# A hybrid block on one core: residual additions moved to TensorE and ScalarE, and other costs in the kernel's planner

## Chip, core and metric

The kernel runs on one core of one Trainium2 chip. The metric is the device time of one execution in microseconds (us), as the median of several runs. TensorE is called PE below, VectorE DVE, ScalarE ACT, GpSimd POOL, and SP is the engine that only issues transfers.

## What is computed

The input x is 8 sequences of 512 tokens of 128 features, float32. The reference, cut to its frame:

```python
def reference(x, ...):
    x = x + delta_rule_attention(layernorm(x))   # "a": 16 heads of 8, short convolution, recurrence over time
    x = x + experts(layernorm(x))                # "f": top 2 of 8 experts, 128 -> 256 -> 128, relu
    x = x + linear_attention(layernorm(x))       # "b": elu+1 features, causal, chunked
    x = x + experts(layernorm(x))                # "g": the same weights as f
    return x
# experts:
#   topw, topi = top_k(softmax(x @ Wg), 2); topw = topw / sum(topw)
#   out = sum over the two chosen e of topw[e] * (relu(x @ W1[e]) @ W2[e])
```

All of it is in float32 except where only signs or counts matter.

## The kernel before

Time is cut into eight chunks of 64 steps; a chunk holds 512 tokens (8 sequences by 64 steps) and lives in SBUF as a tile `x_a` of 128x4x128 values, the residual stream of that chunk. Every chunk passes through four parts: `prepare` and the recurrence (names ending in `_a`, `st`, `pj`, `terms`, `po`), then the experts f, the linear attention b and the experts g. Four lanes work on different chunks at once. Chunk 7 is cut in two halves of 256 tokens.

The experts (`moe`) sort rows: each row is scaled for its two experts (`m_xw`) and sent by indirect transfers from POOL to the table `there` in HBM, ordered by expert. Blocks of 128 rows come back (`m_xs`), are turned by PE (`s_pt`), multiplied with the weights of their expert (`s_ph`, ACT's relu into `hT`, `y_py`) and stored to the table `back`. Then two sets of four indirect gathers bring the two results of every row into two tiles `m_g` (128x512 each), and DVE adds each to `x_a`. The two halves of chunk 7 and one part, g of chunk 6, use all experts for all rows instead (`all_experts`) and gather nothing. So there are 13 parts that gather: 7 of f and 6 of g.

The projections of both attentions end in `add_projected`: PE multiplies with Wo into a PSUM bank `s_po`, with a product of a row of ones for the bias in b, and DVE adds the bank to `x_a`.

The program is one straight stream per engine. Its order is not written by hand: `Weaver` is a planner that runs while the program is built. Each part is a generator, a stream, that says before each step which engine it wants next; the planner keeps a clock for every engine, adds the time that `duration` gives for each instruction, and picks, among the steps that could start soonest, the one with the largest value of `chains` (how long before the end the step must start) plus `FAVOURED` (a hand-set bonus by part and chunk). `AHEAD_OF` says how much later than the earliest a step may start and still be picked. `PLANS` and `PASSES` run the planner several times without issuing anything, to make `chains`. What the planner believes is thus never a wait in the program; it decides the order on each engine.

There is one thing more that the planner writes into the program. Where it believes that PE is going to be idle, `keep_busy` fills most of the gap with products of ones that nobody reads (`busy`, 128x512, bf16):

```python
if gap < 0.6 or not banks.free:
    return
...
n = int(BUSY * gap / 0.22)        # BUSY = 0.7
```

Each engine executes its stream in order, so such a product stands in front of whatever comes next on PE. What `duration` says of PE (`took(engine, us, lag)` takes the time on the engine and the lag until another engine sees the result) is therefore also what decides how many of them there are.

Of the kernel before, what the change touches and what calls it, by code (L numbers as in the profile page):

```python
# [14 lines left out]
ALU = mybir.AluOpType  # L15
# [4 lines left out]
P = 128  # L20
# [19 lines left out]
PREPARED_ON_POOL = ()  # L40
VALUES_ON_POOL = ()
ADDED_ON_PE = ()
AHEAD_OF = 0
PLANS = 4

LANDS = 3.4
ROWS_LAND = 3.8

PASSES = (
    (1, 0.0, {}),  # L50
    (35, 0.1, {}),
)

FAVOURED = {
    ("b", 0): 365, ("b", 3): 20, ("b", 4): 25, ("b", 5): -8, ("b", 6): -10, ("b", 7): -22, ("b", 7.5): 10,
    ("beside",): -5,
    ("ending",): 4,
    ("f", 0): -43, ("f", 1): 17, ("f", 2): -3, ("f", 3): -3, ("f", 4): -3, ("f", 5): 15, ("f", 6): 309, ("f",
    7): -32, ("f", 7.5): 29,
    ("g", 0): -5, ("g", 3): -13, ("g", 4): -37, ("g", 5): -2, ("g", 6): -15, ("g", 7): 321, ("g", 7.5): 170,  # L60
    ("prepare", 0): -5, ("prepare", 1): -2, ("prepare", 2): -22, ("prepare", 3): 10, ("prepare", 5): -6,
    ("prepare", 7): -10,
    ("recur", 0): 105, ("recur", 1): 98, ("recur", 2): -19, ("recur", 3): -7, ("recur", 4): 10, ("recur", 5):
    -47, ("recur", 6): 15, ("recur", 7): -28,
    ("values",): 14,
}

HALVED = (7,)
# [28 lines left out]
class Weaver:  # L97
# [69 lines left out]
    def spawn(self, steps, part=None):  # L167

        ended = Event()

        def run():
            yield from steps
            ended.at, ended.causes = self.seen(), self.waited()

        of = self.stream
        self.live.append(Stream(self.state(), (of.key, of.spawned), part or of.part, run()))
        of.spawned += 1
        return ended
# [154 lines left out]
class Timed:  # L333
# [5 lines left out]
    def __getattr__(self, op):  # L339
        call = getattr(self.engine, op)  # L340

        def issue(*args, **kw):
            r = call(*args, **kw)  # L343
            self.weaver.took(*duration(self.key, op, args, kw))
            return r

        return issue


def free_size(ap):  # L350
    n = 1
    for d in ap.shape[1:]:
        n *= d
    return n


def duration(key, op, args, kw):
    if op == "dma_start":
        return key, 0.4, 0.0, None, LANDS
    if op == "value_load":  # L360
        return key, 0.75, 0.0
    if op == "indirect_dma_start":
        return key, 1.3, 0.0, None, ROWS_LAND
    if key == "PE":
        if op == "transpose":
            return key, 0.2, 0.15
        return key, max(free_size(args[2]) * 1.75e-3, 0.27), 0.15
    out = args[0] if args else kw["out"]
    n = free_size(out)
    if op == "tensor_reduce":  # L370
        n = free_size(args[1])
    if key == "ACT":
        table = TABLE_OF.get(args[2]) if op == "activation" else None
        return key, (0.39 if "bias" in kw else 0.2) + n * 0.76e-3, 0.1, table
    if key == "POOL" and ALU.pow in args:
        return key, 1.05, 0.1
    if key == "POOL":
        return key, 0.15 + n * (1.8e-3 if n > 512 else 2.2e-3), 0.1
    if op == "reciprocal":
        return key, 0.15 + n * 6.5e-3, 0.0  # L380
    if op == "bn_stats":
        return key, 0.28, 0.0
    return key, 0.16 + n * 1.04e-3, 0.0
# [3 lines left out]
def kernel(ctx: ExitStack, tc: tile.TileContext, *tensors: bass.AP):  # L387
# [9 lines left out]
    for n, ahead, favoured in PASSES:  # L397
        for _ in range(n):
# [3 lines left out]
            chains.update(weaver.before_end())  # L402
    merged(ctx, tc, Weaver(chains, FAVOURED, AHEAD_OF), *tensors)


def merged(
# [40 lines left out]
    spawn = weaver.spawn  # L447
    pe = Timed(weaver, nc.tensor, "PE")
    dve = Timed(weaver, nc.vector, "DVE")
    act = Timed(weaver, nc.scalar, "ACT")  # L450
# [25 lines left out]
    ident = const.tile([P, P], F32, name="ident")  # L476
# [38 lines left out]
    def by_row(at):  # L515
        return None if isinstance(at, Shape) else bass.IndirectOffsetOnAxis(ap=at, axis=0)
# [16 lines left out]
    def held_in(n, shape, key, pool_=slots):  # L533
        return Slots(weaver, pool_, shape, key, n)

    banks = held_in(GENERAL, [P, 512], "s", ps)
# [101 lines left out]
    def all_of(events):  # L638
        for e in events:
            yield e  # L640
# [587 lines left out]
    def moe(xt, name, tag):  # L1228
# [7 lines left out]
        held, m_ = helds[own], ms[own]  # L1236
        pl = yield from long_banks.take(f"pl_{name}")
        yield "PE"
        for j in range(nb):
            pe.matmul(  # L1240
                pl[:, j * (NE + 1) : (j + 1) * (NE + 1)], xnT[:, j * P : (j + 1) * P], wg,
                start=True, stop=True,
# [191 lines left out]
        for g in range(0, NBK, 4):  # L1434
            n = min(4, NBK - g)
# [48 lines left out]

            stored.append(spawn(put()))
        yield from all_of(stored)
        added = []
        for k in range(2):
            g = yield from m_.take(f"g_{name}_{k}")
            for at in range(HB):  # L1490
                yield "POOL"
                pool.indirect_dma_start(
                    out=g[:, at, :], out_offset=None, in_=yd,
                    in_offset=by_row(rows[:, k * HB + at : k * HB + at + 1]),
                )
                back = weaver.now
                weaver.now -= ROWS_LAND

            def add(g=g, back=back):
                weaver.goes_on(back)  # L1500
                yield "DVE"
                dve.tensor_tensor(xt, xt, g, ALU.add)
                m_.give(g)

            added.append(spawn(add()))
        yield from all_of(added)
        sets.give(own)

    def add_projected(xt, lhsT, w, name, bias=None):
        nb = xt.shape[1]  # L1510
        po = yield from banks.take(f"po_{name}")
        yield "PE"
        whole = name in ADDED_ON_PE
        rows = xt.rearrange("p b d -> p (b d)")
        if whole:
            pe.matmul(po[:, 0 : nb * D], ident, rows, start=True, stop=False)
        if bias is not None:
            pe.matmul(
                po[:, 0 : nb * D].rearrange("p (b d) -> p b d", b=nb), ones1,
                bias.unsqueeze(1).to_broadcast([1, nb, D]), start=not whole, stop=False,  # L1520
            )
        start = not whole and bias is None
        for j in range(nb):
            pe.matmul(
                po[:, j * D : (j + 1) * D], lhsT[:, j], w, start=start, stop=start or j + 1 == nb
            )
        if whole:
            yield "ACT"
            act.copy(rows, po[:, 0 : nb * D])
        else:  # L1530
            yield "DVE"
            dve.tensor_tensor(rows, rows, po[:, 0 : nb * D], ALU.add)
        banks.give(po)
# [127 lines left out]
    def linear_attention(c, lo, xt, tag):  # L1661
        nb = xt.shape[1]
        n = f"b{c}_{lo}"
        if c > 0:
            yield from all_of([fired("att", c - 1, i) for i in rows_of(c - 1)])
        xnT_ = yield from xns.take(f"xnT_{n}")
        xnT = xnT_.rearrange("p b d -> p (b d)")
        yield from transposed(xt, xnT, n)
        pm = yield from banks.take(f"pm_{n}")
        yield "PE"  # L1670
        for j in range(nb):
            pe.matmul(
                pm[:, j : j + 1], xnT[:, j * P : (j + 1) * P], wg[:, NE:], start=True, stop=True
            )
        mean = small.tile([P, HB], F32, tag="mean" + tag, name=f"mean_{n}")[:, 0:nb]
        yield "ACT"
        act.copy(mean, pm[:, 0:nb])
        banks.give(pm)
        rs = yield from inverse_deviation(xt, mean, n, tag)
        nrs = small.tile([P, HB], F32, tag="nrs" + tag, name=f"nrs_{n}")[:, 0:nb]  # L1680
        yield "POOL"
        pool.tensor_scalar(nrs, rs, -1.0, None, ALU.mult)

        att = yield from xns.take(f"att_{n}")
        fire("att", c, lo)
        yield from all_of([spawn(attend(c, lo, j, xnT, rs, nrs, att)) for j in range(nb)])
        yield from transposed(att[:, 0:nb], xnT, f"t_{n}")
        xns.give(att)
        yield from add_projected(xt, xnT_, wob, f"b{c}" if nb == HB else n, bob)
        xns.give(xnT_)  # L1690
# [16 lines left out]
    def of_rows(c, lo, nb, tag):  # L1707

        n = f"{c}" if nb == HB else f"{c}_{lo}"
        part = c + lo / HB  # L1710
        xt = xts[c][:, lo : lo + nb]
        yield ("f", part)
        yield from add_projected(xt, oTs[c][:, lo : lo + nb], woa, f"a{n}")
        fire("added", c, *([] if nb == HB else [lo]))
        yield from moe(xt, f"f{n}", tag)
        yield ("b", part)
        yield from linear_attention(c, lo, xt, tag)
        yield ("g", part)
        yield from moe(xt, f"g{n}", tag)
        yield "SP"  # L1720
        for i in range(2):
            sp.dma_start(in_units(out, c, i)[:, lo : lo + nb], xt[i * CH : (i + 1) * CH])
# [71 lines left out]
```

## Time and profile before

| | |
|---|---|
| median of 3 runs | 951.38 us (951.37 to 951.84) |
| the profiled execution | 1007.78 us, its span 1006.1 us |
| mean granted PE clock in the profile | 0.919 |
| busy: PE, PE weight loads, DVE, ACT, POOL | 83%, 54%, 65%, 52%, 47% of the span |
| instructions | 14877, of them 4144 products on PE, each with its weight load |
| `busy` products | 514 |

The profiled execution is longer than the median run: 1007.78 against 951.38. Durations below are of the profiled execution, from its first to its last instruction. A float32 product is two instructions on PE, a transpose or a bf16 product is one. The busy time of PE counts each product from its start to its modelled end, so a product that is followed closely by another is counted in part while the next already runs: what a product takes away from others is seen better in the distance between starts. The instructions of the program nearly all carry the line of one helper (L343), so groups are told apart by the names of their tiles; the `busy` products have a line of their own, L1735.

### The profile page before, as it was taken

The page shows a single profiled execution, that of the slowest core. Times are in us where ns is not written, and L with a number is a line of the kernel's source. Part 1 is how long each engine was busy: PE and PEld are TensorE (multiplying, and loading weights), DVE is VectorE, ACT ScalarE, POOL GpSimd, SP SyncE. Part 2 cuts the span into 40 slices and gives each one's busy share as a digit, 9 for nine tenths or more (in the row PEclk, how much of TensorE's full clock was granted, in tenths as well). Part 3 has the DMA queues.
Part 4 walks back from the last instruction along what each step waited for, and adds up shares of the span by engine and source line. Part 5 has one row for each costly group of instructions (what it writes and reads, how often), then busy time and mean ns, then how long its engine had stood idle before and what let it go on. Part 6 is the DMA issues. An engine that isn't in the chain of part 4 may idle for free.

```text
span 1006.1 us, 14877 instructions
## 1 busy us (share of the span) xinstructions
PE 834.4 (83%) x4144; PEld 540.9 (54%) x4144; DVE 655.4 (65%) x1625; ACT 523.7 (52%) x1464; POOL 476.3 (47%) x615
## 2 busy tenths in 40 slices
PE   8978697688898887888787788779876848999998
PEld 3332242537453676447643575547745737776566
DVE  1377878648898487788788796688774812264520
ACT  4343255665656456765385475753752526435343
POOL 1133136254646434774367635774366442554530
PEclk9989799799899789899988898989998969999999
DMA  1404504586206464367615574763635636611111
GB/s 27 101 21 116 159 6 127 159 228 189 57 4 178 126 204 129 96 174 222 164 53 161 161 223 126 197 190 102 202 113 155 201 107 169 170 54 48 37 48 38
DMA packets 157989, 126.83 MB, mean 126 GB/s; under 512 B 53105, under 2 KB 123730, under 8 KB 157906
## 3 DMA queue, kind: packets, MB, share of 16 engines
q1 hardware_dynamic: 150674, 112.16, 39.6%
q0 software_dynamic: 6656, 13.64, 4.7%
q8 instruction: 33, 0.54, 0.2%
q14 instruction: 50, 0.41, 0.1%
q10 hardware_dynamic: 576, 0.08, 0.0%
HBM read 91.70 MB, written 36.23 MB: 127 GB/s over the span
## 4 chain that ended last, share of the span: by engine, by line
PE 37%; DVE 28%; ACT 11%; issue 7%; DMA 5%; POOL 5%; another core or an unknown queue 4%; SPq 2%; ACTq 0%; DVEq 0%; POOLq 0%
PE s_ph_g L343 5%; PE y_py_g L343 5%; PE y_py_f L343 4%; PE s_pc_b L343 4%; PE s_pu_b L343 3%; PE s_ph_f L343 3%; DVE st L343 3%; ACT squares L343 3%; DVE factors L343 3%; PE s_pp_a L343 2%; POOL po L343 2%; DVE terms L343 2%; SPq L343 2%; DVE pj L343 2%
## 5 line engine op out<-in xcount | busy, mean ns | idle before, releaser
L1735 PE MATMUL busy<-ones 128*128 128x512 bf16 x514 | 131.5, 403 | 5.3 <-DVE sbd L343 2.4
L343 POOL TENSOR_TENSOR po<-st,kq 128x256 f32<-128x256 f32 x128 | 94.8, 768 | 5.7 <-DVE o L343 5.5
L343 PE MATMUL s_pp_a<-xnT_a,wc 128*128 128x512 f32 x192 | 92.6, 621 | 0.6 <-ACT xnT_a L343 0.6
L343 POOL COPY st<-st 128x64 f32<-128x64 f32 x31 | 8.0, 257 | 175.9 <-DVE st L343 165.5
L1735 PEld LDWEIGHTS <-ones 128*128 128x128 bf16 x514 | 52.1, 104 | 71.3 <-issue 27.2
L343 POOL TENSOR_TENSOR kv_b<-ph_b,v 128x1024 f32<-128x1024 f32 x32 | 63.1, 1974 | 56.8 <-DVE ph_b L343 31.7
L343 PE MATMUL y_py_f<-wt_f,hT_f 128*128 128x128 f32 x420 | 64.7, 308 | 21.5 <-ACT hT_f L343 19.7
L343 ACT ACTIVATE hT_g<-s_ph_g 128x512 f32<-128x512 f32 (+1 forms) x96 | 48.5, 511 | 62.8 <-PE s_ph_g L343 38.2
L343 DVE TENSOR_REDUCE st<-terms 128x64 f32<-128x320 f32 x128 | 62.1, 485 | 24.8 <-ACT terms L343 7.9
L343 ACT COPY terms<-st 128x64 f32<-128x64 f32 x128 | 39.5, 309 | 74.5 <-DVE st L343 64.8
L343 PE MATMUL s_pc_b<-kv_b,tri 128*128 128x512 f32 x128 | 69.7, 648 | 10.3 <-POOL kv_b L343 6.7
L343 PEld LDWEIGHTS y_py_f<-wt_f,hT_f 128*128 128x128 f32 x420 | 58.6, 218 | 28.0 <-ACT hT_f L343 23.6
L343 POOL DMA_INDIRECT there<-m_xw_f,rows_f x56 | 55.9, 999 | 34.2 <-ACT m_xw_f L343 17.6
L343 ACT ACTIVATE hT_f<-s_ph_f 128x512 f32<-128x512 f32 (+1 forms) x88 | 43.7, 501 | 52.8 <-PE s_ph_f L343 38.7
L343 POOL DMA_INDIRECT m_g_f<-back,rows_f x56 | 56.1, 1002 | 31.3 <-issue 15.1
L343 PE MATMUL y_py_g<-wt_g,hT_g 128*128 128x128 f32 x360 | 50.3, 288 | 20.9 <-issue 11.1
L343 DVE TENSOR_REDUCE o<-po 128x64 f32<-128x512 f32 x64 | 42.9, 679 | 34.5 <-POOL po L343 34.5
L343 PE MATMUL s_ph_f<-xsT_f,wt_f 128*128 128x128 f32 x420 | 60.7, 298 | 5.5 <-ACT xsT_f L343 4.5
L343 DVE TENSOR_REDUCE factors<-pj 128x32 f32<-128x288 f32 x128 | 58.8, 460 | 7.4 <-ACT factors L343 3.8
L343 PEld LDWEIGHTS s_ph_f<-xsT_f,wt_f 128*128 128x128 f32 x420 | 56.5, 211 | 10.5 <-ACT xsT_f L343 6.3
L343 PEld LDWEIGHTS s_pp_a<-xnT_a,wc 128*128 128x128 f32 x192 | 36.2, 198 | 43.8 <-issue 37.7
L343 PE MATMUL s_ph_g<-xsT_g,wt_g 128*128 128x128 f32 x360 | 52.2, 296 | 9.0 <-ACT xsT_g L343 3.4
(312 smaller groups left out, 1989.3 us busy)
## 6 DMA issues: line engine op xcount, KB each, us to landing
wt_f<-w SPq DMA_DIRECT2D x105, 256.0 KB
wt_g<-w SPq DMA_DIRECT2D x90, 256.0 KB
scr<-y_a SPq DMA_DIRECT2D x24, 256.0 KB
m_xs_f<-there SPq DMA_DIRECT2D x21, 256.0 KB
back<-yb_f SPq DMA_DIRECT2D x21, 256.0 KB
m_xs_g<-there SPq DMA_DIRECT2D x18, 256.0 KB
back<-yb_g SPq DMA_DIRECT2D x18, 256.0 KB
qk<-scr SPq DMA_DIRECT2D x16, 256.0 KB
```

What stands on the lines that cost most here:

```text
L343: r = call(*args, **kw)
L1735: nc.tensor.matmul(pt, ones, ones.unsqueeze(1).to_broadcast([P, 4, P]), start=True, stop=True)
```

## The change

`add_projected` always adds the residual rows by a product with the identity into the same bank, ahead of the others, and ACT copies the bank back to `x_a`. In `moe` both gathers are awaited together; then PE adds `x_a` and both gathered tiles by three products with the identity into a bank `s_pg`, and ACT copies it to `x_a`. The planner gets other costs for PE: 0.9 ns for a column instead of 1.75, a least time of 0.05 us instead of 0.27, a transpose like a product of 128 columns (0.115 us instead of 0.2), widths between 128 and 256 taken as 256, and a lag of 0.3 us instead of 0.15. `AHEAD_OF`, `PASSES` and `FAVOURED` have other values.

```diff
-AHEAD_OF = 0
+AHEAD_OF = 0.15
@@
 PASSES = (
     (1, 0.0, {}),
-    (35, 0.1, {}),
+    (17, 0.0, {}),
 )
 
 FAVOURED = {
-    ("b", 0): 365, ("b", 3): 20, ("b", 4): 25, ("b", 5): -8, ("b", 6): -10, ("b", 7): -22, ("b", 7.5): 10,
...
-    ("values",): 14,
+    ("b", 5): 159, ("b", 6): -3, ("b", 7): 28, ("b", 7.5): 27,
...
+    ("recur", 0): 74, ("recur", 1): 36, ("recur", 4): 2, ("recur", 7): 1,
+    ("values",): -5,
 }
@@ def duration(key, op, args, kw):
     if key == "PE":
-        if op == "transpose":
-            return key, 0.2, 0.15
-        return key, max(free_size(args[2]) * 1.75e-3, 0.27), 0.15
+
+        n = P if op == "transpose" else free_size(args[2])
+        n = 2 * P if P < n < 2 * P else n
+        return key, max(n * 0.9e-3, 0.05), 0.3
@@ def moe(xt, name, tag):
-        added = []
+        both = []
         for k in range(2):
             g = yield from m_.take(f"g_{name}_{k}")
             for at in range(HB):
...
-                back = weaver.now
                 weaver.now -= ROWS_LAND
-
-            def add(g=g, back=back):
-                weaver.goes_on(back)
-                yield "DVE"
-                dve.tensor_tensor(xt, xt, g, ALU.add)
-                m_.give(g)
-
-            added.append(spawn(add()))
-        yield from all_of(added)
+            both.append(g)
+        weaver.goes_on(weaver.now + ROWS_LAND)
+
+        po = yield from banks.take(f"pg_{name}")
+        flat = xt.rearrange("p b d -> p (b d)")
+        yield "PE"
+        pe.matmul(po, ident, flat, start=True, stop=False)
+        for k in range(2):
+            pe.matmul(po, ident, both[k].rearrange("p b d -> p (b d)"), start=False, stop=(k == 1))
+            m_.give(both[k])
+        yield "ACT"
+        act.copy(flat, po)
+        banks.give(po)
         sets.give(own)
@@ def add_projected(xt, lhsT, w, name, bias=None):
-        whole = name in ADDED_ON_PE
+        whole = True
```

`ADDED_ON_PE` was empty before, so no projection was added on PE.

More of the change, by code (lines that the diff above doesn't have):

```diff
@@ L50 @@
     (1, 0.0, {}),
-    (35, 0.1, {}),
+    (17, 0.0, {}),
 )
 FAVOURED = {
-    ("b", 0): 365, ("b", 3): 20, ("b", 4): 25, ("b", 5): -8, ("b", 6): -10, ("b", 7): -22, ("b", 7.5): 10,
[L56 to L64, printed above, removed]
-    ("values",): 14,
+    ("b", 5): 159, ("b", 6): -3, ("b", 7): 28, ("b", 7.5): 27,
+    ("beside",): 5,
+    ("f", 3): 50, ("f", 4): 4, ("f", 5): -5, ("f", 6): -5, ("f", 7): -17, ("f", 7.5): 104,
+    ("g", 3): 1, ("g", 4): -30, ("g", 5): -53, ("g", 6): 48, ("g", 7): -16, ("g", 7.5): -6,
+    ("prepare", 0): -5, ("prepare", 1): 3, ("prepare", 3): -10,
+    ("recur", 0): 74, ("recur", 1): 36, ("recur", 4): 2, ("recur", 7): 1,
+    ("values",): -5,
 }
```

## The prediction, made before the changed kernel was run

> **What bounds the kernel now.** I read the page first. No engine is full over the whole span, and the chain that ended last goes through all of them: PE has 37% of it, DVE 28%, ACT 11%.
>
> ```profile
> span 1006.1 us, 14877 instructions
> PE 834.4 (83%) x4144; PEld 540.9 (54%) x4144; DVE 655.4 (65%) x1625; ACT 523.7 (52%) x1464; POOL 476.3 (47%) x615
> PEclk9989799799899789899988898989998969999999
> PE 37%; DVE 28%; ACT 11%; issue 7%; DMA 5%; POOL 5%; another core or an unknown queue 4%; SPq 2%; ACTq 0%; DVEq 0%; POOLq 0%
> ```
>
> See here that DVE, from which the change takes work, carries a smaller part of the chain than PE, to which it gives work. Next I asked for stretches of 50 us: all of PE's instructions, then those of the tile `busy` alone (its last three numbers are granted clock, DMA share and GB/s).
>
> ```profile
> 300.00:350.00 50.00, 42.82 (x165) 24.63 (x165) 32.81 (x88) 28.05 (x71) 28.52 (x30) 0.86 0.51 142
> 950.00:1000.00 50.00, 49.57 (x210) 34.69 (x208) 8.93 (x45) 22.62 (x63) 12.56 (x20) 1.00 0.15 41
> ...
> 150.00:200.00 50.00, 18.50 (x74) 0.86 0.53 141
> 300.00:350.00 50.00, 0.59 (x2) 0.86 0.51 142
> 650.00:700.00 50.00, 0.00 (x0) 0.89 0.50 149
> ```
>
> See that the program has two regimes. Up to 200 us the recurrence runs nearly alone and the plan fills PE with `busy` products (about 370 of the 514). From 200 us on it puts in few (147 in 800 us): it believes PE to be full there. The last 150 us are PE at its limit already.
>
> Third, the timeline around 430 us, for what one product costs:
>
> ```profile
> 429.54 0.59 PE L343 MATMUL s_pp_a<-xnT_a,wc 128*128 128x512 f32 x1
> 430.80 1.02 PE L343 MATMUL s_pc_b<-kv_b,tri 128*128 128x512 f32 x2
> 432.80 0.39 PE L343 MATMUL s_pk_b<-ph_b,tri 128*128 128x128 f32 x2
> 435.41 1.24 PE L1735 MATMUL busy<-ones 128*128 128x512 bf16 x5
> ```
>
> A float32 product is two passes (x2). At 512 columns one pass shows 0.59 us, and two show 1.02: the passes start 0.43 apart, so the product keeps PE for 0.86 us. At 128 columns two passes end after 0.39; elsewhere eight passes take 1.05, so (1.05 - 0.27)/7 = 0.11 a pass, 0.22 a product. Five bf16 products take 1.24: (1.24 - 0.38)/4 = 0.215 each.
>
> **The change, part by part.**
>
> *The additions.* The rows that go or have a model:
>
> ```profile
> L343 DVE TENSOR_TENSOR x_a<-x_a,m_g_f 128x512 f32<-128x512 f32 x14 | 13.6, 973 | 2.6 <-DMA m_g_f<-back,rows_f 2.6
> L343 DVE TENSOR_TENSOR x_a<-x_a,m_g_g 128x512 f32<-128x512 f32 x12 | 9.0, 748 | 11.0 <-DMA m_g_g<-back,rows_g 11.0
> L343 DVE TENSOR_TENSOR x_a<-x_a,s_po_b 128x512 f32<-128x512 f32 x7 | 4.8, 681 | 6.2 <-PE y_py_g L343 4.3 <-PE s_po_b L343 1.8
> L343 ACT COPY yb_f<-y_py_f 128x512 f32<-128x512 f32 x21 | 12.2, 582 | 20.9 <-PE y_py_f L343 10.3 <-remote 7.8 <-PE s_ph_f L343 2.2
> ```
>
> DVE loses 13.6 + 9.0 us for the gathered rows, and 2 x 4.8 us and four halves of 0.42 for the projections: 33.9 us. At DVE's 28% of the chain that is worth 9 us. PE gains 13 x 3 products of 0.86 = 33.5 us and 14 x 0.86 + 4 x 0.43 = 13.8 us, together 47 us; at its 37% this costs 17 us. ACT gains 27 copies of 0.58 and four of 0.38: 17.2 us, 2 us at its 11%. Per part with gathers, what follows the last gather was one DVE addition, 0.68 us; it becomes a product (1.02) and a copy (0.58), 0.9 us more. Four such parts lie one behind another in a lane at most; I take 4 us, between 0 (other lanes cover it) and 13 x 0.9 = 12. No transfer is added, moved or taken away, and POOL and SP issue what they did, in the new order.
>
> *The moved wait.* DVE waited 13.6 us for gathered rows; now PE does, and behind the waiting product stand the products of all other lanes. The row gives 13.6 as one end; the other is 0, if the rows land before the products' turn, as they did for 23 of 26 additions. I take 4 us, because the plan still allows 3.8 us for landing. So the additions by themselves come to -9 + 17 + 2 + 4 + 4 = +18 us at most, if PE is as tight as its share says. The first 200 us and PE's gaps, 124 us between 200 and 850 by its busy time, hide part: I take +8, with ends -9 (only DVE's relief counts) and +18.
>
> *The planner's costs.* This is the large part. The change says that the plan now knows the distance of PE's products. The trace says otherwise for wide ones: a 512-column product is seen after 1.02 us; the old plan said 0.896 + 0.15 = 1.046, the new one says 0.461 + 0.3 = 0.761. At 128 columns the trace has 0.39, the old plan 0.42, the new one 0.415. And the time that a product keeps PE was right (0.896 against 0.86; 0.27 against 0.22) and becomes half of the truth (0.461; 0.115): the new figure fits one pass, and a float32 product has two.
>
> What the plan thinks of PE after 200 us, from the counts of the groups there (passes halved): 183 products of 512 columns, 836 of 128, 188 of 144, 32 of 384, 138 of 256, 380 transposes, 143 small ones. With the old costs 164 + 226 + 51 + 22 + 62 + 76 + 39 = 640 us of the 806; with the new ones 84 + 96 + 43 + 11 + 32 + 44 + 7 = 317, and 25 for the new products: 342. Its free time on PE goes from 166 us to 464, and `keep_busy` fills gaps. Today the 147 fillers take 147 x 0.22 = 32 us, 20% of the free time, since most gaps are under 0.6 us. With three times the free time over about the same number of steps (some 750), the mean gap grows from 0.22 to 0.62 us. If gaps are spread exponentially, gaps over 0.6 hold 75% of the free time and rounding leaves 61% of them filled: 45%. That is 209 us, 950 fillers after 200 us instead of 147. The ends are 20% (the share of today: 420) and 70% (all gaps long: 1480). With the fillers of the start I expect about 1350 in all, between 800 and 1850.
>
> What PE then really has to do after 200 us, at full clock, by the distances between starts: 183 x 0.86 = 157, 836 x 0.22 = 184, 188 x 0.30 = 56, 32 x 0.60 = 19, 138 x 0.44 = 61, 380 x 0.11 = 42, the small ones 23: 542 us. Fillers today 147 x 0.215 = 32: 574 of 806, 71%. Afterwards 542 + 46 + 950 x 0.215 = 792, 98%. PE can't be used to 98% where its products wait for ACT and DVE in between; I estimate 93%, between the busy share of the middle (about 0.82) and the last stretch (0.99). 792/0.93 = 852 us instead of 806: +46. This already contains the new products and a clock at its full rate. With the ends of the filler count: 420 give 678 us, which fits; 1480 give 906, +168.
>
> *The clock.* The trace has a granted clock of 0.86 to 0.97 in the middle and 1.00 in the last 150 us, where PE never rests. The Trainium skill, "TensorE: Matmul & The Clock Gate", in the table under "Why this matters for your kernels", asks for no idle gaps over some 3 us between bursts, since an idle window halves the clock; by this rule more fillers are a gain. By the row, a clock of 0.91 instead of 1 costs 542 x (1/0.91 - 1) = 54 us of PE time, at 37% of the chain 20 us. By the rule alone the sum would be +8 - 20 = -12; by the row for the fillers it is +46, with the clock already counted as full. I go by the row, since a filler of 0.215 us takes its time from PE whether the clock needed it or not.
>
> *Order.* `FAVOURED`, `PASSES` and `AHEAD_OF` make another order on all engines. No row shows the price. I bound it by 25 us on both sides, the size of single entries in the list of waits (ACT for `s_ph_f` 38.7 in all, DVE for `s_pc_b` 17.5), and take -4: steps that may start 0.15 us later but matter more can win a little.
>
> **Sum.** +46 - 9 (DVE's relief, not contained in PE's sum) + 2 + 4 - 4 = +39 us on 1006. The median run is 951.38/1007.78 = 0.944 of the profiled one, so +37: 988 us. The fill share is a guess, and slightly lower shares count more, since they leave no overflow: I name 984.
>
> **The rivals.**
>
> *Warm and relieved (faster).* The fillers stay in time that PE really has free. It decides at 542 + 46 + fillers below 0.93 x 806 = 750 us, that is under 750 fillers after 200 us, a fill share of 35%. Then the clock's 20 us and DVE's 9 are gained, against 2 for ACT and 4 for later rows: -23 on 1006, -22: 929 us. For it: holes in the clock row (0.76 from 800 to 850). Against: free time by the plan nearly triples, and 35% is reached early.
>
> *Nothing much.* Fillers at today's share, +8 for the additions, a clock a little better (-8): 951 us.
>
> *Overflow (much slower).* A fill share of 55%, 1160 fillers: 542 + 46 + 249 = 837, /0.93 = 900, +94 on 1006, with the rest +82: 1029 us. For it: `busy` bursts already stand on the chain of today (26 of them, 5.7 us, at 32 us; 1.43 us at 435), though the old plan knew PE well. Against: fillers need a free bank.
>
> *Does it do what it says?* The rows show that the plan's distance gets worse for wide products; that the additions do move is certain from the code.
>
> **How the numbers follow.** A change under 0.2% (2 us) can't be told from none in this measurement. PE overfilled by a part, about 984: 0.52; overflow, about 1029: 0.18; warm and relieved, about 929: 0.18; little either way, about 951: 0.12, of which a third each falls on slower, same and faster. So slower 0.74, same 0.04, faster 0.22. The likeliest case alone runs from 958 to 1010. To hold 8 in 10 the range reaches into both others: 933 to 1042.
>
> **What would show it.** `busy` products: 1350 (800 to 1850), most of the new ones between 200 and 850 us, where there are 147 from 200 us to the end now. PE's busy share over 90%, its granted clock over 0.95, its share of the chain up, with `busy` as a line of its own in it. DVE's rows `x_a<-x_a,m_g` and `x_a<-x_a,s_po` gone, 34 us; ACT rows `x_a<-s_pg` and `x_a<-s_po` of 0.58 us each; 39 and 18 products of the identity on PE, the wide ones with passes 0.43 us apart. PE idle for a gather some 4 us in all. I am wrong if the fillers number under 800, or if they are there and the time still falls: then the clock or the new order is worth more than the room that they take.

## The result, and the profile after

The changed kernel takes 1023.97 us (1019.85 to 1025.25, 3 runs), 1.0751 times the time before (95% interval 1.0703 to 1.0799). In a second measurement (e5) it was 1022.57 against 944.8 us: 1.082 (1.074 to 1.090). The forecast was 984, so the sign was right and the loss, 73 us, more than twice the 33 us that were forecast.

The kernel before takes 945 to 951 us on some occasions and about 1000 us on others, whatever the experiment beside it. In its two profiles of the second kind 4% of the chain stands at "another core or an unknown queue", time in which an engine stands still and the profile names nothing that it waits for; the first profile was of that kind. These are called stalls below. Every ratio is to runs of the kernel before made beside the experiment, on the same chip. For comparing traces a second profile of the kernel before (e16, span 945.8 us) stands beside one of the changed kernel (e5), both without those stalls. The page of the second profile of before: span, the engines' row, clock, chain by engine.

```profile
span 945.8 us, 14877 instructions
PE 813.5 (86%) x4144; PEld 527.1 (56%) x4144; DVE 654.2 (69%) x1625; ACT 522.9 (55%) x1464; POOL 477.6 (50%) x615
PEclk9989789899989999799999998979899999999999
PE 36%; DVE 30%; ACT 10%; POOL 7%; DMA 7%; issue 6%; SPq 3%; DVEq 0%; ACTq 0%; POOLq 0%
```

The same of the changed kernel (e5), with its `busy` row:

```profile
span 1019.9 us, 15854 instructions
PE 921.3 (90%) x4634; PEld 577.1 (57%) x4634; DVE 627.2 (61%) x1581; ACT 536.9 (53%) x1491; POOL 471.9 (46%) x615
PEclk9989799999999988998999889899999999999999
PE 65%; DVE 18%; ACT 6%; issue 4%; DMA 3%; POOL 3%; SPq 1%; ACTq 0%; DVEq 0%; POOLq 0%
L1735 PE MATMUL busy<-ones 128*128 128x512 bf16 x890 | 218.8, 390 | 7.5 <-DVE ph_b L339 3.7 <-DVE qs_b L339 2.4 <-ACT y_a L339 0.7
```

See that PE's share of the chain goes from 36% to 65%, while its clock is better (0.960 against 0.945 on the mean). The fillers, which is what the `busy` products are called here, rise from 514 to 890 only. The moved additions themselves look as they were costed, in the groups by form of e5:

```profile
L339 PE MATMUL s_pg_f<-m_g_f,ident 128*128 128x512 f32 x28 | 14.2, 621 | 1.7 <-DMA m_g_f<-back,rows_f 1.7
L339 ACT COPY x_a<-s_pg_f 128x512 f32<-128x512 f32 x7 | 4.1, 585 | 16.2 <-PE s_pg_f L339 16.2
```

and one part's three products in its chain in order of time (start, length):

```profile
602.82 2.58 PE s_pg_f L339 x6
```

Six passes take 2.58 us, 0.43 each; a copy 0.585. PE idles 1.7 us for gathered rows, where DVE idled 16.2 in the second profile of before (first two rows below). But the wait has not gone: ACT now stands at the additions, all at PE's products (the four rows after them), 78 us in all, where DVE's `x_a` additions had waited 31 us for gathered rows and projections together.

```profile
DVE x_a L343 <- DMA m_g_g<-back,rows_g: 10.3, 2, 9.8
DVE x_a L343 <- DMA m_g_f<-back,rows_f: 5.9, 2, 3.2
...
ACT x_a L339 <- PE s_po_a L339: 27.2, 8, 10.8
ACT x_a L339 <- PE s_po_b L339: 22.3, 9, 3.4
ACT x_a L339 <- PE s_pg_f L339: 16.2, 6, 5.3
ACT x_a L339 <- PE s_pg_g L339: 12.0, 6, 3.2
```

In these rows, as in those below, the numbers are the sum of the waits, how many, and the longest.

Where the time goes is seen in the list of waits. Before (e16):

```profile
ACT hT_g L343 <- PE s_ph_g L343: 38.0, 54, 1.8
DVE qs_b L343 <- PE s_pc_b L343: 14.9, 12, 6.8
DVE sbd L343 <- PE s_pu_b L343: 14.6, 22, 2.2
ACT y_a L343 <- PE s_pp_a L343: 5.1, 2, 2.8
```

After (e5):

```profile
ACT hT_g L339 <- PE s_ph_g L339: 60.5, 71, 4.7
DVE qs_b L339 <- PE s_pc_b L339: 36.8, 37, 4.0
DVE sbd L339 <- PE s_pu_b L339: 49.7, 36, 5.9
ACT y_a L339 <- PE s_pp_a L339: 25.9, 12, 4.0
```

None is long (6.8 us at most before, 5.9 after). There are many more of them after: ACT and DVE come to PE's results too early, 156 times in these four rows instead of 90, and in their queues other work stands behind. In time, the recurrence of the two kernels is still within 15 us at its chunk 5 (DVE's `on` of it starts at 567 and at 582 us), and then it starves. The windows of 0 to 200, 200 to 600, 600 to 750 and 750 to 940 us were compared; here is the third of each kernel, before first (PE, PE's loads, DVE, ACT, POOL busy; clock, DMA share, GB/s):

```profile
600.00:750.00 150.00, 133.05 (x778) 100.33 (x777) 124.50 (x305) 87.37 (x244) 97.85 (x108) 0.92 0.63 189
600.00:750.00 150.00, 134.88 (x745) 88.78 (x744) 91.57 (x237) 84.84 (x236) 78.28 (x92) 0.97 0.55 159
```

PE is as busy there as before; DVE, which carries the recurrence, has 92 us of work instead of 125. Chunk 6 of the recurrence, counted between the starts of DVE's `on` of chunks 5 and 6, takes 151 us (582 to 732) where it took 95 (567 to 662). DVE's other work had fallen behind earlier: between 200 and 600 us it has 297 us of work instead of 332, and only 19 us of the difference are additions that the change takes from it.

### The profile page after: what moved, and what is told of

Its sections match the earlier page's. It is cut to its first block, busy times and chain, and to the rows that moved or that the text cites. A ratio compares the mean times of both kernels' runs of the same rounds, so it can differ in the third digit from the quotient of the medians.

```text
span 1023.5 us, 15854 instructions
## 1 busy us (share of the span) xinstructions
PE 927.6 (91%) x4634; PEld 581.3 (57%) x4634; DVE 626.1 (61%) x1581; ACT 537.3 (52%) x1491; POOL 473.2 (46%) x615
## 4 chain that ended last, share of the span: by engine, by line
PE 65%; DVE 17%; ACT 6%; issue 4%; DMA 3%; POOL 3%; SPq 2%; ACTq 0%; DVEq 0%; POOLq 0%
PE s_pp_a L339 8%; PE y_py_g L339 7%; PE s_ph_g L339 7%; PE busy L1735 6%; PE s_ph_f L339 5%; PE y_py_f L339 5%; PE s_pc_b L339 5%; PE s_pu_b L339 4%; PE s_po_b L339 2%; PE s_pS_b L339 2%; PE s_pn_a L339 2%; DVE W L339 2%; SPq L339 2%; PE s_pg_g L339 2%; PE s_po_a L339 1%
## 5 line engine op out<-in xcount | busy, mean ns | idle before, releaser
L1735 PE MATMUL busy<-ones 128*128 128x512 bf16 x890 | 221.3, 394 | 7.5 <-DVE ph_b L339 3.7
L1735 PEld LDWEIGHTS <-ones 128*128 128x128 bf16 x890 | 89.2, 102 | 107.5 <-issue 29.5
L339 POOL TENSOR_TENSOR po<-st,kq 128x256 f32<-128x256 f32 x128 | 89.6, 727 | 3.4 <-DVE o L339 3.3
L339 PE MATMUL s_pp_a<-xnT_a,wc 128*128 128x512 f32 x192 | 88.4, 602 | 0.7 <-ACT xnT_a L339 0.7
L339 DVE TENSOR_TENSOR qs_b<-s_pc_b,ph_b 128x512 f32<-128x512 f32 x64 | 43.5, 687 | 37.5 <-PE s_pc_b L339 37.1
L339 PE MATMUL s_ph_f<-xsT_f,wt_f 128*128 128x128 f32 x420 | 57.4, 287 | 5.0 <-ACT hT_f L339 4.1
L339 POOL DMA_INDIRECT there<-m_xw_g,rows_g x48 | 48.9, 1019 | 23.4 <-ACT m_xw_g L339 10.9
L339 DVE TENSOR_TENSOR pj<-st,factors 128x256 f32<-128x256 f32 x128 | 53.5, 418 | 9.3 <-ACT factors L339 5.4
L339 DVE TENSOR_TENSOR terms<-factors,kt 128x256 f32<-128x256 f32 x128 | 54.1, 423 | 7.1 <-ACT factors L339 3.0
L339 POOL DMA_INDIRECT m_g_g<-back,rows_g x48 | 47.7, 995 | 19.6 <-issue 12.7
```

Source lines behind the costliest of these rows:

```text
L1735: nc.tensor.matmul(pt, ones, ones.unsqueeze(1).to_broadcast([P, 4, P]), start=True, stop=True)
```

## The experiments

Theories at the start: the wrong costs of PE's products (with the fillers they bring), the additions, the order (other `FAVOURED`, `PASSES`, `AHEAD_OF`). `AHEAD_OF` alone was not run.

**One part alone.** e1, the costs alone:

```diff
+        n = P if op == "transpose" else free_size(args[2])
+        n = 2 * P if P < n < 2 * P else n
+        return key, max(n * 0.9e-3, 0.05), 0.3
```

> The kernel before with nothing changed but the planner's costs of PE (0.9 ns a column, least 0.05 us, lag 0.3). Theory of the costs (the plan takes float32 products for half as long as they are, so it orders steps wrongly and puts fillers into time that PE does not have): most of the 73 us are here, 990 to 1025 us, with some 350 to 450 more fillers and PE above 60% of the chain of waits. Theory of the additions (products of the identity and the gather wait on PE cost it): 945 to 960 us, whatever the filler count. Theory of the order (the other FAVOURED, PASSES and AHEAD_OF): 945 to 965 us.

Measured 1134.77 us, ratio 1.1333 (1.1271 to 1.1396): more than the whole change, and outside all that was expected. It has 1290 fillers, and PE is 60% of its chain.

e2, the gathered rows alone on PE, and e3, the projections alone:

```diff
-                dve.tensor_tensor(xt, xt, g, ALU.add)
+            pe.matmul(po, ident, both[k].rearrange("p b d -> p (b d)"), start=False, stop=(k == 1))
...
+        act.copy(flat, po)
```
```diff
-        whole = name in ADDED_ON_PE
+        whole = True
```

> The kernel before with only the gathered rows added by three products on PE and a copy by ACT; costs, FAVOURED and projections as before. Theory of the costs: 948 to 962 us (33.5 us more on PE, 22.6 less on DVE). Theory of the additions: 985 us or more, with PE idle for gathers for over 10 us and x_a late for its followers. Theory of the order: a plan for which FAVOURED was not made, so anything from 951 to 970.

> The kernel before with only the projections added on PE (one product of the identity more, ACT copies). Theory of the costs: 948 to 958 us (13.8 us more on PE, 11 less on DVE). Theory of the additions: 965 us or more. Theory of the order: 951 to 970.

Measured 1.0542 (1.0476 to 1.0609) for e2 and 1.0117 (1.0081 to 1.0153) for e3. By itself e2 looks like the price of the additions; the orders below show that it can't be read so.

e8, the three settings alone, no instruction and no cost changed:

```diff
+AHEAD_OF = 0.15
+    (17, 0.0, {}),
+FAVOURED = { ... }   # of the changed kernel
```

> The kernel before with only FAVOURED, PASSES and AHEAD_OF of the changed one; costs and additions as before. Theories A and B: 1.00 to 1.03. Theory C: 1.03 to 1.06, that is as much as the gathered additions alone gave, so that those 5% would be a plan without its FAVOURED, not the additions.

Measured 1.0721 (1.0641 to 1.0801), above what any theory had expected: nearly as much as the whole change (1.082 beside it), with none of its additions or costs. Its instructions are those of the kernel before, but for the fillers (747).

**The fillers left out.** e4 keeps the changed kernel's plan and doesn't issue the fillers:

```diff
-            for _ in range(n):
-                nc.tensor.matmul(
-                    pt, ones, ones.unsqueeze(1).to_broadcast([P, 4, P]), start=True, stop=True
-                )
```

> The changed kernel with the fillers planned as they are but not issued: the same order of everything else, 890 products fewer on PE. If the time went to the fillers themselves (445 us-long bursts in front of useful products, 467 x 0.215 = 100 us after 200 us): 950 to 975 us. If it went to the order that the wrong costs make, or to the additions: 1010 to 1040 us, since the clock also falls (below 0.9) when PE rests.

Measured 1.0845 (1.0806 to 1.0883), against 1.075 and 1.082 with them. With the clock that they bring counted in, the fillers are not where the time goes. Their absence shows in the clock (its row, its mean, and the chain):

```profile
PEclk9658579688759998968999599988869966999999
core 0: 1076.6 us, clock 0.848
PE 56%; DVE 18%; ACT 10%; issue 6%; POOL 4%; DMA 3%; another core or an unknown queue 2%; SPq 1%; ACTq 0%; DVEq 0%; POOLq 0%
```

PE is still 56% of the chain. What a filler costs and what the clock gains by it are seen only together here; that each by itself is small is not shown.

**The change with one part undone.** e5 is the changed kernel again, as the yardstick; e6 has the old costs; e7 only doubles the planned time of every product that is not a transpose, since nearly all of them are float32 and take two passes:

```diff
-        return key, max(n * 0.9e-3, 0.05), 0.3
+        passes = 1 if op == "transpose" else 2
+        return key, max(n * 0.9e-3, 0.05) * passes, 0.3
```

> The changed kernel itself, on the same chip as the next three, as their yardstick: a ratio of 1.075 to the kernel before, as in the first measurement; if ratios depend on the chip, 1.05 to 1.09.

> The changed kernel with the old costs of PE in the plan (1.75 ns a column, 0.27 us, lag 0.15); additions, FAVOURED, PASSES and AHEAD_OF as changed. Theory A (the wrong costs make an order in which DVE and ACT wait for PE's products): a ratio of 1.01 to 1.04, better than the changed kernel although FAVOURED was not made for these costs. Theory B (the additions on PE are what costs; the gathered ones alone gave 1.054): 1.05 to 1.08. Theory C (the plan lives from a FAVOURED made for it, any other combination loses 3 to 5%): 1.06 to 1.12.

> The changed kernel with one edit in the plan's costs: a float32 product is two passes, so its time on PE is doubled (0.92 us at 512 columns, 0.23 at 128); the lag stays 0.3. Theory A (it is the halved time of the products): 1.01 to 1.05, with fewer than 700 fillers. Theory B (additions): 1.05 to 1.08. Theory C (FAVOURED not made for it): 1.06 to 1.12.

Measured 1.082 (1.074 to 1.090) for e5, 1.0779 (1.0705 to 1.0853) for e6, 1.0871 (1.0789 to 1.0954) for e7. Taken from here, the costs seem to be worth nothing; from e1 they are worth 13%. Both can't be the price of one thing, unless the settings fit one of them. e6 and e8 differ in the additions alone (1.0779 against 1.0721): no price of the additions that this can tell.

**Is an order worth 7%?** e9 has only `FAVOURED` of the changed kernel, e10 only its `PASSES`, e11 only `LANDS = 3.5` for 3.4, e15 34 passes for 35:

> The kernel before with only FAVOURED of the changed one; PASSES, AHEAD_OF, costs and additions as before. If the 7% of the three settings together are FAVOURED made for another plan: 1.04 to 1.08. If they are PASSES or AHEAD_OF: 0.99 to 1.02.

> The kernel before with only PASSES of the changed one: 17 planning passes with no allowance in place of 35 with 0.1 us. If FAVOURED fits only the plan it was made on: 1.03 to 1.07, since the values of chains differ. If the passes only refine a plan that is good anyway: 0.99 to 1.02.

> The kernel before with LANDS = 3.5 instead of 3.4, the plan's time for a transfer to land; nothing else, and no instruction added or taken. It tells how far an order moves the time when no cost gets worse. If the time before is one order picked out of many by its measured time: 1.03 to 1.07, like the gathered additions alone (1.054). If the order is robust, and the additions did cost their 1.054 by themselves: 0.99 to 1.015.

> The kernel before with 34 planning passes instead of 35 of the same kind, nothing else. If the order before is one picked out of many: 1.03 to 1.08 (FAVOURED was fitted to the 35th). If e11 was an accident of its nudge: 0.99 to 1.015.

Measured 1.0489 (1.0429 to 1.0549) for e9, 1.0767 (1.0703 to 1.0831) for e10, 1.0720 (1.0659 to 1.0780) for e11, 1.0312 (1.0259 to 1.0364) for e15. A tenth of a microsecond in the plan's idea of a transfer, with the same instructions but for the fillers, brings 7% (e11), though not all of it by the order, as the next traces show. All eight orders on the old costs that differ from the one before, with or without additions (e2, e3, e6, e8, e9, e10, e11, e15), are slower than it, between 1.012 and 1.078, on the mean 1.056.

e12 and e16 are the kernel before, for its profile:

> The kernel before, unchanged, for a profile on the same chip as the others: if its execution is about 950 us, the stalls of the first profile (4% of its chain at another core or an unknown queue) are gone, and PE's share of the chain is still under 45%. If it is about 1000 us, they are there again.

> The kernel before, unchanged, for a profile beside the other three: at the time of this chip, 945 to 1005 us; the last addition of part a near 0.83 of its span as in the other profile of it (824 of 992.8 us).

e12 took 994.53 us with 4% of its chain in the stalls named above, e16 947.49 us with none; PE's share is 38% and 36%. The chains of e12 and of e11, measured beside it, and then ACT at one pair of instructions in the first profile of before and in e12:

```profile
PE 38%; DVE 27%; ACT 11%; issue 7%; DMA 5%; POOL 4%; another core or an unknown queue 4%; SPq 3%; DVEq 0%; ACTq 0%; POOLq 0%
PE 36%; DVE 29%; ACT 9%; issue 9%; another core or an unknown queue 5%; POOL 5%; DMA 3%; SPq 2%; DVEq 0%; ACTq 0%; POOLq 0%
...
818.06 0.60 ACT L343 ACTIVATE hT_g<-s_ph_g 128x512 f32<-128x512 f32 x1 [11.24 <-remote]
823.87 0.60 ACT L343 ACTIVATE hT_g<-s_ph_g 128x512 f32<-128x512 f32 x1 [4.74 <-remote]
...
804.64 0.60 ACT L343 ACTIVATE hT_g<-s_ph_g 128x512 f32<-128x512 f32 x1 [9.68 <-remote]
811.78 0.60 ACT L343 ACTIVATE hT_g<-s_ph_g 128x512 f32<-128x512 f32 x1 [6.07 <-remote]
```

The stalls come back at the same instructions, so how long they are belongs to the program, and a ratio to another program need not take them out. Together, "issue" and "another core or an unknown queue" are 151 us of e11's chain, 103 of e12's and 55 of e16's. Of the 75 us between e11 and e12, 48 lie there; by this estimate its order alone would cost some 3%. e10 and e2 have 141 and 145 us there, so their ratios are likewise too high; the chains of e3 and e9 can't be followed to their start. What stands without this doubt is what was measured where neither kernel stalls: e15 with 1.031, e8 with 1.072 and e6 with 1.078.

**The same nudge to the changed kernel.** e13 is the changed kernel with `LANDS = 3.5`; e14 is the changed kernel with the additions back on DVE:

> The changed kernel with LANDS = 3.5 instead of 3.4 in the plan. If its order was picked out of many like the one before: 1.11 to 1.16 of the kernel before (1.03 to 1.07 of the changed one). If it is an order like any other: 1.05 to 1.11, to either side of 1.08.

> The changed kernel with the additions back on DVE (residual rows, gathered rows), its costs and settings kept. If the additions have a price of their own: under 1.06. If only the order counts: 1.06 to 1.11.

Measured 1.1521 (1.1461 to 1.1582) for e13 and 1.1471 (1.1423 to 1.1519) for e14, which is outside both its ranges; neither has the stalls. An order is called fitted here when its settings suit it alone, so that small departures from it are slower. By these two the changed kernel's order is a fitted one as well, and with its fit disturbed it stands about where e1 stands. The additions are not what keeps it from the time before: without them (e14) it is slower still.

**What the wrong costs cost.** e17 is e13 with a third of each burst of fillers; e18 is e13 with the two passes of e7:

```diff
-            for _ in range(n):
+            for _ in range(-(-n // 3)):
```

> The kernel of e13 (changed kernel, LANDS 3.5) with the same plan, but each burst of fillers cut to a third of its length, rounded up: some 450 instead of 1197. If the fillers are what the wrong costs cost (some 500 fewer after 200 us, 0.215 us each, 105 us of PE, at its 66% of the chain 70 us): about 1.08. If it is the order, and fillers only keep the clock up: 1.14 to 1.17.

> The kernel of e13 with the costs doubled for float32 products (two passes), the lag of 0.3 kept: a second order of this kind beside e7 (1.087). If the halved products are the price of the new costs: 1.05 to 1.10, under 900 fillers. If the lag or the small products are: 1.13 to 1.17.

Measured 1.1551 (1.1473 to 1.1630) for e17 and 1.0584 (1.0542 to 1.0627) for e18. Of e13, e17 and e18, the `busy` row and the chain:

```profile
L1735 PE MATMUL busy<-ones 128*128 128x512 bf16 x1197 | 294.7, 394 | 20.4 <-DVE ph_b L339 8.3 <-ACT y_a L339 6.4 <-DVE qs_b L339 5.4
PE 66%; DVE 18%; ACT 7%; DMA 3%; issue 3%; POOL 2%; SPq 1%; DVEq 0%; ACTq 0%; POOLq 0%
...
L1735 PE MATMUL busy<-ones 128*128 128x512 bf16 x437 | 137.8, 439 | 19.0 <-DVE ph_b L339 7.4 <-ACT y_a L339 6.4 <-DVE qs_b L339 3.2
PE 57%; DVE 17%; ACT 9%; issue 6%; POOL 4%; DMA 3%; SPq 3%; another core or an unknown queue 1%; ACTq 0%; DVEq 0%; POOLq 0%
...
L1736 PE MATMUL busy<-ones 128*128 128x512 bf16 x759 | 194.5, 405 | 21.2 <-issue 12.1 <-DVE qs_b L339 7.8 <-ACT y_a L339 1.3
PE 39%; DVE 32%; ACT 9%; issue 7%; POOL 5%; another core or an unknown queue 4%; DMA 2%; SPq 2%; DVEq 0%; ACTq 0%; POOLq 0%
```

A third of the fillers leaves the ratio where it was, with the clock at 0.862 instead of 0.963. The true length of a product takes 8% off it and brings PE back to 39% of the chain. e17, e18 and e4 were measured where there are stalls; the two entries are 85, 112 and 82 us of their chains, 44 to 54 us more than in e13, e7 and e5, which have the same kind of order without stalls. The kernel before has 48 us more, so these three ratios are good to about 1%. The waits are shorter with the true length too, here e13 and then e18:

```profile
DVE qs_b L339 <- PE s_pc_b L339: 62.2, 45, 16.9
ACT hT_f L339 <- PE s_ph_f L339: 55.9, 68, 3.0
...
DVE qs_b L339 <- PE s_pc_b L339: 38.6, 27, 8.9
ACT hT_f L339 <- PE s_ph_f L339: 28.6, 41, 2.0
```

**The account.** That order and not work makes the loss is shown: the settings alone bring 1.072 (e8), leaving out fillers gains nothing (e4, e17), and the additions make no difference that can be told (e6 against e8). How the loss divides is argued from few orders. Two effects of about equal size and opposite sign seem to hide each other. The new costs cost some 8%: the three orders on them without a fit stand at 1.133, 1.147 and 1.152, mean 1.144; those on the old costs without a fit at 1.056 on the mean, and the two with products of two passes at 1.058 and 1.087. By the runs without stalls alone it is 1.147 and 1.152, against 1.031, 1.072 and 1.078 (mean 1.060), and 1.087 with two passes. The changed kernel's settings, in its own plan, get back 6 to 7% of it (1.152 to 1.082). What is left is about the advantage that the order before has over its neighbours, 1.06, and some 2% more. The orders of one kind scatter by 3%, and the sizes are no better than that.

## Why the prediction was right and wrong, by its steps

*The additions* (+8 us, between -9 and +18): agrees, as far as it can be told. e6 against e8 gives 1.0779/1.0721, +5 us, with overlapping intervals. Copies of 0.585 us and passes of 0.43 are as written. DVE's busy time fell by 27 us (654.2 to 627.2).

*The moved wait* (4 us): 1.7 us in the row of `s_pg_f`, none in that of `s_pg_g`. The step asked only for PE's wait; ACT's, 78 us at PE's products, it did not see. With the old costs in the plan (e6) the same four rows of ACT sum to 37 us, so most of the growth over DVE's 31 comes with the costs.

*What the plan believes*: right, and it was the most useful step. The costs take a float32 product for one pass; mending only that takes e13 from 1.152 to e18's 1.058. In the changed kernel itself it gains nothing (e7, 1.087 against 1.082), which fits if mending also undoes the fit.

*The number of fillers* (1350, 800 to 1850; 950 of them after 200 us): 890, and 467 after 200 us. The orders on the same costs without a fit have 1290, 1197 and 1161 (e1, e13, e14), near the estimate; the fitted order has fewer.

*The price of the fillers* (+46 us through 98% of PE): this step failed. It priced a filler by the PE time that it takes, as if PE's fullness set the time. With 467 fillers the sum of that step would have been (542 + 46 + 100)/0.93 = 740 us of 806, no loss at all, and the kernel lost 73. Leaving all of them out (e4) or two thirds (e17) moves the ratio by no more than 1%, and not downwards. The Trainium skill's rule, "TensorE: Matmul & The Clock Gate", under "Why this matters for your kernels", that gaps between bursts lower the clock, agrees in its direction: 0.960 with all fillers, 0.848 with none. What the fillers take and what the clock gives come to nothing together, and the step counted only the taking. Most of the signs that were named came (890 fillers, PE busy for 90%, clock 0.960, PE's share of the chain up), and yet they don't carry the loss: e4, with no filler, PE busy for 74% and a clock of 0.848, loses as much.

*Order* (-4 us, 25 on either side): the term that was mis-sized, and the one that holds the loss. Settings that change nothing but the order and the fillers are worth 28 us (e15) to 70 us (e8), and the wrong costs most likely work through the order too: ACT and DVE are sent to wait at products that keep PE twice as long as planned. The trace of before could not show the first; but the prediction had the second in its hands, 0.761 us against 1.02, and turned it into fillers only. So the sign came out right in part by luck: the plan's error was seen, but the way in which it was to cost time is not the way in which it did.

*The rivals.* Overflow named 1029 us (its own sum, 951 + 82, gives 1033), which is near, for a reason that e4 and e17 exclude. Warm and relieved had a better clock and a relieved DVE; both came, and the time rose all the same. That the plan would know PE's distances worse was right.

*The scale* of 0.944 between the profile and the median was no property of profiling: the profile of before held stalls, and the runs of the median most likely had none (e16's profile, without stalls, took 947.49 us). It moved the forecast by 2 us.

## What to carry to other kernels

Where a planner writes the order, a changed cost is a changed program: ask first what each engine's queue will now stand at, and only then how many instructions it adds. An order that was fitted can be worth several per cent that no row of its profile shows, so compare a change with other orders too, by a nudge that should mean nothing (here one planning pass fewer, or 0.1 us in a landing time), before a part of it is called good or bad. Look at the stalls of both traces before a ratio is put down to the order. Count the passes of a product before a duration from a trace goes into a model.

## What was not expected of the hardware

The kernel answers to order far more than to work: the same instructions, but for fillers, take 1.072 times as long where nothing stalls (e8). A 512-column pass of float32 started 0.43 us after the one before it at the median of every profile, and 0.85 us after it where the granted clock stood at a half; still, a mean clock of 0.848 instead of 0.960 was made up for by 890 fillers fewer, to about 1%. The stalls came and went between measurements, on the same chip too (chip 10 gave 1001.83 us and 949.96 us for the kernel before), and fell on the same instructions when they came; their cause stays open.

What stays open besides: how the fitted orders were found, and which placements in them carry the gain. The window of 600 to 750 us shows only where the changed kernel falls behind.
